# Layer 2's row ends: no transposes back, diagonal and residual in halves beside the cell's gates

## The chip, the cores and the metric

The kernel runs on one core of a Trainium2 chip, as one launch. The metric is the device time of that launch in microseconds (us). The engines are named as in the profile: PE is TensorE (matmuls and transposes; PEld is its loading of weights), DVE is VectorE, ACT is ScalarE, POOL is GpSimd, SP is SyncE, which only issues DMAs here. A name with a q (SPq, ACTq) is an engine's sequencer. All arithmetic is in fp32, apart from some masks in bfloat16.

## The reference

There are N = 2708 nodes with F = 256 features, and a dense matrix `adj` of N x N that has no negative entries and holds about 1% nonzeros. Four graph layers follow one another, and each is wrapped in a residual and a layernorm without gain and offset:

```python
x = layernorm(x + L0(x, adj))          # adj @ (x * W)
x = layernorm(x + L1(x, adj, ...))     # attention with 4 heads of 64
x = layernorm(x + L2(x, adj, adj, ...))
x = layernorm(x + L3(x, adj, ...))
```

The change lies between layers 2 and 3. Cut to what matters, with the branches for negative entries left out:

```python
# L2(h)
dn = de = diag(adj);  A = adj with its diagonal set to 0
edge_output = gru(A @ h, h, edge weights)
support     = mean over 3 heads of softmax(masked scores) * A @ (h @ gat_W)
node_output = gru(support, h, node weights)
return de[:, None] * edge_output + dn[:, None] * node_output
# L3(x)
hn = adj @ (x @ neigh_W.T) / (adj.sum(1, keepdims=True) + 1)
return concatenate([x, hn], axis=-1) @ lin_W.T
```

Layer 3 is linear in x, so it can be written as `x @ L1 + rdeg * (adj @ (x @ L2))`, where L1 is the first half of `lin_W.T`, L2 is `neigh_W.T` times its second half, and rdeg is 1 / (degree + 1). The kernel uses that: `lwn` is the matrix of 256 x 512 that holds L1 and L2 side by side.

## The kernel before

**Tiles.** The nodes lie in NT = 22 row tiles of P = 128 (the last has 20). The features are FC = 2 halves of 128. Two layouts are in use: rows (a node on each partition, 256 features in the free dimension) and transposed (128 features on the partitions, nodes in the free dimension).

**Layer 2's heads.** The output columns are split into two halves h of NH = 1354 nodes, and each of these into three units u of 512, 512 and 330 columns. One unit takes both halves at once. The loop at the end of this section runs over the units, over the K = 3 heads and over the MH = 11 pairs c of row tiles. For each pair, ACT makes the scores `p` with two activations (L1258 and L1261), DVE multiplies them by the block of `adj` (L1262), and `seven` (L298) forms one product of 2 x 2 blocks with seven matmuls in place of eight: DVE makes the sums `s` and `pa` (L304 to L307) for it, and L317 issues the matmuls into seven of the eight PSUM banks. So L317 is the stream that PE works on throughout this stage, from 887 to 1626 us, with two breaks in it for other work at each pair.

**Turns.** After the third and the sixth of the seven matmuls `seven` calls `between` (L291). It runs one step of a Python generator, up to its next `yield`: first from the list `urgent`, and if this is empty, from `later`. One such step is a turn. A unit with 3 x 11 pairs has 66 turns. `project` (L1098, 4 turns for each head) goes into `urgent`; `edge_cells` (L1233) and `node(u, est)` (L1208) go into `later`. So `node(0)` runs in the turns of unit 1's heads, `node(1)` in those of unit 2's, and `node(2)` in those of layer 3's first unit, where some pairs have a turn after each of their seven matmuls. The turns set the order of PE's instructions; on the other engines the order in which the program's lines are reached, together with the Tile scheduler, decides.

**One bank for all turns.** `bank()` (L1057) hands out the one PSUM bank that is left (the pool `ps_f` has one buffer). Each turn takes it, PE writes it, and ACT or DVE must have read it before the next turn's first matmul may start.

**node.** For each half h of a unit (six halves in all):

1. `load_cell` (L1184) loads `xt`, the transposed features of the layer's input, and `et`, the edge cell's output, by DMAs that POOL issues (L246). Each has one buffer. For h = 1 this stands in the loop over the row ends of h = 0.
2. `cell` (L1115) computes the GRU cell, transposed, in 8 turns: for each half j of the features the gates r, h, n and z, each with two or four matmuls (L1128) and one ACT activation out of the bank. The DVE operations that combine the gates stand after the fourth gate, and write `yt`.
3. L1217 adds `et` to `yt` for both halves of features in one DVE operation.
4. `by_tiles` (L1191) cuts the columns into row tiles. A tile that reaches over the border between two stretches of columns is put together by POOL copies (L1201).
5. The row ends take three turns for each of the 22 tiles. `node_rows` (L1152) transposes `yt` back to rows (two PE transposes, L1157); DVE reads the bank, multiplies by the node's diagonal entry and adds the residual `xs` (L1160), and the layernorm follows: statistics on DVE, the power for 1/sqrt on POOL, the normalisation on DVE (L181). `rows_turned` (L1166) transposes the normalised rows again (two PE transposes, L1170), and ACT copies them to `xt` (L1172). `rows_end` (L1175) multiplies them by `lwn` (two matmuls with 512 columns, L1179); ACT copies the second half to `h3` (L1180), DVE adds the first half to the normalised rows (L1181), and POOL issues the DMA that stores this sum as `y3_d` for the end of layer 3.

**Layer 0's stage** prepares `lwn`: `lin_W` and `neigh_W` are transposed, multiplied (L559) and stored to memory; `load_lwn` loads the result ahead of layer 2's heads. `diag`, the diagonal in rows layout (128 x 22), is there from that stage on. The stage that transposes the softmax statistics stands at about 700 to 720 us and writes them to `st_d`.

Of the kernel before, what the change touches and what calls it, by code (L numbers as in the profile page):

```python
# [19 lines left out]
P = 128  # L20
# [7 lines left out]
def kernel(  # L28
# [113 lines left out]

    fall_d = dram.tile([H, N], F32, name="fall_d")
    st_d = [dram.tile([2 * K, 2, W], F32, name=f"st_{u}") for u in range(len(units))]

# [247 lines left out]
    if True:  # L393
# [13 lines left out]
        if True:  # L407
# [39 lines left out]
            with pool("l0", 2) as l0:  # L447
# [48 lines left out]
                with pool("prep", side="right") as prep:  # L496
# [49 lines left out]
                    nw = weights(prep, "nw", neigh_w)  # L546
                    lw = weights(prep, "lw", lin_w)
                    nc.gpsimd.dma_start(lwn_d[:, :, :F], lw[:, :FC])
                    lwn2 = prep.tile([P, FC, F], F32, name="lwn2")
# [6 lines left out]
                    for i in range(FC):  # L556
                        pt = ps_t.tile([P, 4, P], F32, tag="tr", name="pt").rearrange("p i q -> p (i q)")
                        for o in range(FC):
                            nc.tensor.matmul(  # L559
                                pt[:, :F], nwt[:, o, i * P : (i + 1) * P], lw[:, FC + o, :], start=(o == 0), stop=(o == FC - 1)  # L560
                            )
                        nc.scalar.copy(lwn2[:, i], pt[:, :F])
                    nc.gpsimd.dma_start(lwn_d[:, :, F:], lwn2)
                    layer0_mask(ahead, strips[ahead])
# [42 lines left out]
            if True:  # L607
# [350 lines left out]
                next(ahead)  # L958

                for lo in range(0, NT, 4):  # L960
                    hi = min(lo + 4, NT)
# [84 lines left out]
    with (  # L1046
# [67 lines left out]

        def cell(est, xt, yt, w, wih, whh, b):  # L1115

            for j in range(FC):
                got = {}
                for i, nm in ((0, "r"), (2, "h"), (3, "n"), (1, "z")):
# [9 lines left out]
                    if nm == "n":  # L1129
                        nc.scalar.activation(yt[:, j, :w], g[:, :w], AF.Identity, bias=b[:, 3, j : j + 1])  # L1130
                    else:
                        s = nleft.tile([P, W], F32, tag=f"g_{nm}", name=f"g_{nm}")
                        nc.scalar.activation(
                            s[:, :w], g[:, :w], AF.Identity if nm == "h" else AF.Tanh,
                            scale=0.5, bias=b[:, i, j : j + 1],
                        )
                        got[nm] = s
                    yield

# [6 lines left out]
                nc.vector.scalar_tensor_tensor(z, z, 1.0, h, ALU.add, ALU.mult)  # L1146
                nc.vector.scalar_tensor_tensor(n, z, 0.5, r, ALU.mult, ALU.add)


        shared, shared3 = {}, {}  # L1150

        def node_rows(t, src):  # L1152

            n = sz(t)
            pt = bank()
            for f in range(FC):
                nc.tensor.transpose(pt[:n, f * P : (f + 1) * P], src[:, f, :n], ident)  # L1157
            y = nleft.tile([P, F], F32, tag="y", name="y", bufs=3)

            nc.vector.scalar_tensor_tensor(  # L1160
                y[:n], pt[:n, :F], diag[:n, t : t + 1], xs[t][:n], ALU.mult, ALU.add,
            )
            layernorm(y, y, n)
            return t, y

        def rows_turned(t, y):  # L1166
            n = sz(t)
            pt = bank()
            for f in range(FC):
                nc.tensor.transpose(pt[:, f * P : f * P + n], y[:n, f * P : (f + 1) * P], ident[:n, :n])  # L1170
            xt = nleft.tile([P, FC, P], F32, tag="xt", name="xt", bufs=2)
            nc.scalar.copy(xt[:, :, :n], pt.rearrange("p (f q) -> p f q", q=P)[:, :FC, :n])  # L1172
            return t, y, xt

        def rows_end(t, y, xt):  # L1175
            n = sz(t)
            pz = bank()
            for f in range(FC):
                nc.tensor.matmul(pz[:n], xt[:, f, :n], lwn[:, f, :], start=(f == 0), stop=(f == FC - 1))  # L1179
            nc.scalar.copy(h3[t][:n], pz[:n, F:])  # L1180
            nc.vector.tensor_tensor(y[:n], y[:n], pz[:n, :F], ALU.add)  # L1181
            nc.gpsimd.dma_start(y3_d[t], y[:n])

        def load_cell(lo, w):  # L1184
            got = []
            for parts, tag in ((xt_d, "xt2"), (edge_d.values(), "et")):
                got.append(nleft.tile([P, FC, W], F32, tag=tag, name=tag))
                load_columns(got[-1], parts, lo, w, nc.gpsimd)
            return got

        def by_tiles(lo, w, src, ends, among=range(NT)):  # L1191
# [16 lines left out]
        def node(u, est):  # L1208
# [3 lines left out]
            for h in range(2):  # L1212
                lo = h * NH + a
                xt, et = nxt or load_cell(lo, w)
                yt = nleft.tile([P, FC, W], F32, tag="yt", name="yt")
                yield from cell(est[h], xt, yt, w, *node_w, b_node)
                nc.vector.tensor_tensor(yt[:, :, :w], yt[:, :, :w], et[:, :, :w], ALU.add)  # L1217
                tiles = by_tiles(lo, w, lambda at, n: yt[:, :, at : at + n], shared)
                got, turned = [], []
                for i in range(len(tiles) + 2):  # L1220
                    if i < len(tiles):
                        got.append(node_rows(*tiles[i]))
                        yield
                    if i >= 2:
                        rows_end(*turned[i - 2])
                        yield
                    if 0 < i <= len(tiles):
                        turned.append(rows_turned(*got[i - 1]))
                        yield
# [401 lines left out]
```

## Time and profile before

Three runs took 1880.27, 1880.66 and 1879.21 us, a median of 1880.27.

| what | value |
|---|---|
| profiled execution | 1881.39 us |
| its span in the profile | 1879.3 us |
| instructions | 23102 |
| granted TensorE clock | 0.998 of full speed |
| busy PE, 0 to 890 us (layers 0 and 1, edge cells) | 874.5 of 890 us |
| busy PE, 890 to 1180 us (heads of unit 0 and the first of unit 1) | 289.5 of 290 us |
| busy PE, 1180 to 1735 us (heads with row ends among them) | 544.4 of 555 us |
| busy PE, 1735 to 1879 us (layer 3) | 132.2 of 144 us |
| L1157, transposes to rows | 44 matmuls, 1207.9 to 1719.9 us |
| L1170, transposes back | 44 matmuls, 1213.1 to 1729.9 us |
| L1160, DVE, diagonal and residual of a tile | 22 of 0.478 us |
| L181, DVE, normalisation of a tile's rows | 22 of 0.413 us |
| L1172, ACT, copy of the turned rows | 22 of 0.372 us |
| L1181, DVE, sum of the rows and the first half | 22 of 0.416 us |

How to read it: the span is what the profiler recorded between the first and the last instruction, and the time of the execution is longer by what lies around it. The four rows of busy PE come from stretches of the trace. The durations are medians of one instruction in this one execution. A matmul in fp32 shows as two records, and the end of a record is modelled, so the costs of PE are read from starts rather than from durations. Lists that are given as "waiter, releaser" name the instruction that waited, then the one whose end released it.

### The profile page before, as it was taken

Reading aid. Unit: us, or ns where it says so; the run is one execution under the profiler, and the core shown is the slowest. Engines: PE = TensorE matmul, PEld = TensorE weight load, DVE = VectorE, ACT = ScalarE, POOL = GpSimd, SP = SyncE. Lnnn points to the kernel's source line nnn. Section 1 sums busy time; section 2 is a strip of 40 time slices with the busy share of each in tenths; the row PEclk is TensorE's granted clock in tenths of the full one; section 3 lists DMA queues with packets and bytes.
Section 4 is the critical chain, followed back from the end, with each engine's and each line's share of the span. In section 5 each row is a group of like instructions: output and inputs, shape, how many; then the busy total and the mean of one; then the engine's idle time right before and its main releaser. Section 6 shows DMA issues by size and latency. Waiting matters only on the chain.

```text
span 1879.3 us, 23102 instructions
## 1 busy us (share of the span) xinstructions
PE 1840.5 (98%) x7561; PEld 1035.5 (55%) x7565; DVE 1279.0 (68%) x2280; ACT 689.0 (37%) x1419; POOL 259.9 (14%) x419
## 2 busy tenths in 40 slices
PE   8999999999999999999999999999999999999997
PEld 7788842233345886887444444444445555554555
DVE  5343479999897655654658888776887758744664
ACT  4444410033144203111555665555564555311011
POOL 1211220001012411000011001210200202111111
PEclk9999999999999999999999999999999999999999
DMA  9344410100002657764557665454554445534764
GB/s 298 130 146 146 159 42 1 30 1 12 12 7 74 144 143 188 176 144 113 164 148 207 179 168 147 134 155 115 163 144 114 128 103 134 155 101 109 198 167 123
DMA packets 434204, 235.92 MB, mean 126 GB/s; under 512 B 184182, under 2 KB 421388, under 8 KB 431644
## 3 DMA queue, kind: packets, MB, share of 16 engines
q1 hardware_dynamic: 417438, 207.41, 40.5%
q0 software_dynamic: 7760, 21.20, 3.5%
q10 hardware_dynamic: 8878, 5.76, 1.0%
q8 instruction: 62, 1.02, 0.2%
q14 instruction: 66, 0.54, 0.1%
HBM read 221.61 MB, written 12.65 MB: 125 GB/s over the span
## 4 chain that ended last, share of the span: by engine, by line
PE 83%; DMA 5%; DVE 4%; issue 3%; ACT 2%; POOL 1%; SPq 1%; ACTq 0%; DVEq 0%; POOLq 0%
PE m L317 38%; PE acc L763 11%; PE bank L1128 7%; PE acc L211 7%; PE den L772 6%; PE gate L1003 4%; PE bank L1104 3%; DMA strip<-in_adj_t_dram 2%; PE bank L1179 1%; ACT below L465 1%; DMA p<-in_adj_t_dram 1%; SPq L264 1%; PE pm L419 1%; POOL bn_rs L175 1%; PE pq L929 1%
## 5 line engine op out<-in xcount | busy, mean ns | idle before, releaser
L781 DVE SCALAR_TENSOR_TENSOR p<-fall_b,rise,mask 128x1024 f32<-128x1024 f32 (+1 forms) x264 | 294.0, 1157 | 32.5 <-PE den L772 16.7
L1258 ACT ACTIVATE p<-st,e_neg 128x1024 f32<-128x1024 f32 (+1 forms) x198 | 197.1, 1040 | 193.7 <-PE m L317 186.3
L317 PE MATMUL m<-s,xq 128*128 128x512 f32 (+3 forms) x660 | 230.1, 467 | 0.0
L763 PE MATMUL acc<-p,h 128*64 128x512 f32 (+2 forms) x1056 | 214.5, 548 | 0.2 <-ACT sum L794 0.2
L317 PE MATMUL m<-p,xq 128*128 128x512 f32 (+1 forms) x396 | 182.8, 543 | 0.1
L211 PE MATMUL acc<-turn,strip 128*128 128x257 f32 x792 | 181.5, 379 | 0.0
L1261 ACT ACTIVATE p<-p 128x1024 f32<-128x1024 f32 (+1 forms) x198 | 178.9, 943 | 0.2
L1262 DVE TENSOR_TENSOR p<-p,blk 128x1024 f32<-128x1024 f32 (+1 forms) x132 | 143.6, 1107 | 39.7 <-ACT p L1261 24.3
L317 PE MATMUL m<-p,x 128*128 128x512 f32 (+1 forms) x396 | 167.8, 542 | 0.3 <-DVE supt L334 0.3
L304 DVE TENSOR_TENSOR s<-p 128x512 f32<-128x512 f32 (+3 forms) x132 | 81.1, 615 | 124.3 <-PE m L317 101.0
L317 PEld LDWEIGHTS m<-s,xq 128*128 128x128 f32 x660 | 124.3, 190 | 74.8 <-issue 57.6
L211 PEld LDWEIGHTS acc<-turn,strip 128*128 128x128 f32 x792 | 147.2, 190 | 20.3
L763 PEld LDWEIGHTS acc<-p,h 128*64 128x64 f32 x1056 | 69.8, 136 | 138.2 <-issue 128.6
L317 PE MATMUL m<-s,x 128*128 128x512 f32 (+3 forms) x330 | 127.3, 467 | 0.0
L772 PE MATMUL den<-p,h 128*32 128x512 f32 (+2 forms) x1056 | 117.7, 548 | 0.0
L317 PEld LDWEIGHTS m<-p,xq 128*128 128x128 f32 x396 | 74.6, 190 | 76.0 <-issue 61.4
L317 PEld LDWEIGHTS m<-p,x 128*128 128x128 f32 x396 | 74.4, 190 | 73.6 <-issue 61.2
L465 ACT ACTIVATE below<-strip 128x384 bf16<-128x384 f32 x132 | 78.5, 594 | 72.9 <-DMA strip<-in_adj_t_dram 69.5
L1262 DVE TENSOR_TENSOR p<-p,turn 128x1024 f32<-128x1024 f32 (+1 forms) x66 | 72.2, 1108 | 17.9 <-PE m L317 11.6
L305 DVE TENSOR_TENSOR p<-p 128x512 f32<-128x512 f32 (+3 forms) x132 | 82.4, 625 | 1.9
L307 DVE TENSOR_TENSOR s<-p,s 128x512 f32<-128x512 f32 (+3 forms) x132 | 81.5, 617 | 2.0
L317 PEld LDWEIGHTS m<-s,x 128*128 128x128 f32 x330 | 61.8, 190 | 38.1 <-issue 34.3
(276 smaller groups left out, 2541.1 us busy)
## 6 DMA issues: line engine op xcount, KB each, us to landing
strip<-in_adj_t_dram SPq DMA_DIRECT2D x19, 1408.0 KB, 6.0
blk<-in_adj_t_dram SPq DMA_DIRECT2D x88, 256.0 KB, 3.4
blk<-in_adj_t_dram SPq DMA_DIRECT2D x88, 192.0 KB, 4.0
pa<-in_adj_t_dram SPq DMA_DIRECT2D x110, 128.0 KB, 2.7
turn<-in_adj_t_dram SPq DMA_DIRECT2D x44, 256.0 KB, 3.3
blk<-in_adj_t_dram SPq DMA_DIRECT2D x88, 128.0 KB, 2.5
p<-in_adj_t_dram SPq DMA_DIRECT2D x88, 128.0 KB, 2.6
turn<-in_adj_t_dram SPq DMA_DIRECT2D x44, 192.0 KB, 3.1
```

Of the source, the lines that this page charges most:

```text
L211: nc.tensor.matmul(acc, s[:, c, :n], rhs(c), start=(c == 0), stop=(c == NT - 1))
L305: nc.vector.tensor_tensor(a21, a21, a11, ALU.subtract)
L307: nc.vector.tensor_tensor(s4, a12, s2, ALU.subtract)
L317: nc.tensor.matmul(dst[:, :w], lt, rt, start=start and not (one_bank and i), stop=stop and not (one_bank and i in (1, 2, 5)))
L465: nc.scalar.activation(below[:, : (hi - lo) * P], s[:, lo:hi].rearrange("p c n -> p (c n)"), AF.Relu, scale=-1.0, accum_out=negative[:, BE ...
L763: nc.tensor.matmul(acc[s][i * HD : (i + 1) * HD, :ws], hs[c][:, 2 * q + i, :HD], ps[i][:, p0 : p0 + ws], **flags,)
L772: nc.tensor.matmul(den[j : j + CT, :ws], hs[c][:, 2 * q + i, HD + 1 - CT :], ps[i][:, p0 : p0 + ws], **flags,)
L781: nc.vector.scalar_tensor_tensor(p[:, :w], falls[g // 2][:, 2 * q + i, :w], rise[:, c, 2 * q + i : 2 * q + i + 1], mask[:, c, at : at + w] ...
L1128: nc.tensor.matmul(g[:, :w], lt, rt, start=(q == 0), stop=(q == len(terms) - 1))
L1258: nc.scalar.activation(p[:, :, :w], st_k[:, :, :w], AF.Relu, scale=-1.0, bias=e_neg[:, at, k : k + 1])
L1261: nc.scalar.activation(p[:, :, :w], p[:, :, :w], AF.Exp, scale=-1.0)
L1262: nc.vector.tensor_tensor(p[:, :, :w], p[:, :, :w], blk[:, i, :, :w], ALU.mult)
```

## The change

- `cell` takes two functions. `prepare(j)` is called after the gate h of a half j of the features, and multiplies that half of `et` by the diagonal and adds `xt` to it. `rest(j)` is called at the end of the half, and multiplies the half of `yt` by the diagonal and adds that `et`. So residual and diagonal are applied in transposed layout, 128 x 512 (or 330) at a time; L1217 and the DVE operation L1160 go.
- For this the diagonal is needed along the free dimension: it is transposed to a row once, stored to `diag_d`, and loaded for each half, the same on all partitions, as `drow` (one buffer, by POOL's queue).
- One turn between the cell and the row ends does nothing.
- `node_rows` transposes to rows as before, but ACT copies them out of the bank; the statistics are taken from these rows. `rows_turned` is gone: `rows_end` multiplies the slice of `yt`, which has been transposed all along and isn't normalised, by `lwn`. The scale 1/sqrt of a row is applied to the product after it; the mean drops out, because `centred` has taken the mean over the rows from each column of both matrices in `lwn`. Each row tile takes two turns in place of three.

```diff
--- before.py
+++ after.py
@@ -141,6 +141,7 @@
     nc.gpsimd.memset(turn.rearrange("p (t f) -> p t f", f=FE)[:, :, F:], 1.0)
 
     fall_d = dram.tile([H, N], F32, name="fall_d")
+    diag_d = dram.tile([NT, P], F32, name="diag_d")
     st_d = [dram.tile([2 * K, 2, W], F32, name=f"st_{u}") for u in range(len(units))]
 
     y3_d = [dram.tile([sz(t), F], F32, name=f"y3_{t}") for t in range(NT)]
@@ -545,6 +546,16 @@
                         finish(layer0_rest(l0, t))
                     nw = weights(prep, "nw", neigh_w)
                     lw = weights(prep, "lw", lin_w)
+                    minus = prep.tile([P, P], F32, name="minus")
+                    nc.gpsimd.memset(minus, -1.0 / F)
+
+                    def centred(w):
+                        pt = ps_t.tile([P, 4, P], F32, tag="tr", name="pt").rearrange("p i q -> p (i q)")
+                        for f in range(FC):
+                            nc.tensor.matmul(pt[:, :F], minus, w[:, f, :], start=(f == 0), stop=(f == FC - 1))
+                        nc.vector.tensor_tensor(w, w, pt[:, None, :F].to_broadcast([P, FC, F]), ALU.add)
+
+                    centred(lw[:, :FC])
                     nc.gpsimd.dma_start(lwn_d[:, :, :F], lw[:, :FC])
                     lwn2 = prep.tile([P, FC, F], F32, name="lwn2")
                     nwt = prep.tile([P, FC, F], F32, name="nwt")
@@ -560,6 +571,7 @@
                                 pt[:, :F], nwt[:, o, i * P : (i + 1) * P], lw[:, FC + o, :], start=(o == 0), stop=(o == FC - 1)
                             )
                         nc.scalar.copy(lwn2[:, i], pt[:, :F])
+                    centred(lwn2)
                     nc.gpsimd.dma_start(lwn_d[:, :, F:], lwn2)
                     layer0_mask(ahead, strips[ahead])
                     layer0_own(ahead, strips[ahead])
@@ -957,6 +969,11 @@
                 nc.vector.reciprocal(rdeg, rdeg)
                 next(ahead)
 
+                pt = ps_t.tile([P, 4, P], F32, tag="tr", name="pd")
+                nc.tensor.transpose(pt[:NT, 0, :], diag, ident)
+                drows = tail.tile([NT, P], F32, name="drows", bufs=1)
+                nc.scalar.copy(drows, pt[:NT, 0, :])
+                nc.gpsimd.dma_start(diag_d, drows)
                 for lo in range(0, NT, 4):
                     hi = min(lo + 4, NT)
                     at, w = lo * P, width(lo, hi)
@@ -1112,7 +1129,7 @@
                         nc.vector.scalar_tensor_tensor(e, pw[:, :w], 1.0 / K, e, ALU.mult, ALU.add)
                     yield
 
-        def cell(est, xt, yt, w, wih, whh, b):
+        def cell(est, xt, yt, w, wih, whh, b, prepare=None, rest=None):
 
             for j in range(FC):
                 got = {}
@@ -1135,6 +1152,8 @@
                             scale=0.5, bias=b[:, i, j : j + 1],
                         )
                         got[nm] = s
+                    if nm == "h" and prepare:
+                        prepare(j)
                     yield
 
                 r, z, h, n = got["r"][:, :w], got["z"][:, :w], got["h"][:, :w], yt[:, j, :w]
@@ -1145,6 +1164,8 @@
                 nc.vector.tensor_tensor(h, xt[:, j, :w], r, ALU.subtract)
                 nc.vector.scalar_tensor_tensor(z, z, 1.0, h, ALU.add, ALU.mult)
                 nc.vector.scalar_tensor_tensor(n, z, 0.5, r, ALU.mult, ALU.add)
+                if rest:
+                    rest(j)
 
 
         shared, shared3 = {}, {}
@@ -1156,29 +1177,19 @@
             for f in range(FC):
                 nc.tensor.transpose(pt[:n, f * P : (f + 1) * P], src[:, f, :n], ident)
             y = nleft.tile([P, F], F32, tag="y", name="y", bufs=3)
-
-            nc.vector.scalar_tensor_tensor(
-                y[:n], pt[:n, :F], diag[:n, t : t + 1], xs[t][:n], ALU.mult, ALU.add,
-            )
-            layernorm(y, y, n)
-            return t, y
-
-        def rows_turned(t, y):
-            n = sz(t)
-            pt = bank()
-            for f in range(FC):
-                nc.tensor.transpose(pt[:, f * P : f * P + n], y[:n, f * P : (f + 1) * P], ident[:n, :n])
-            xt = nleft.tile([P, FC, P], F32, tag="xt", name="xt", bufs=2)
-            nc.scalar.copy(xt[:, :, :n], pt.rearrange("p (f q) -> p f q", q=P)[:, :FC, :n])
-            return t, y, xt
-
-        def rows_end(t, y, xt):
+            nc.scalar.copy(y[:n], pt[:n, :F])
+            mean, rs = moments(y, n)
+            return t, src, y, mean, rs
+
+        def rows_end(t, src, y, mean, rs):
+
             n = sz(t)
             pz = bank()
             for f in range(FC):
-                nc.tensor.matmul(pz[:n], xt[:, f, :n], lwn[:, f, :], start=(f == 0), stop=(f == FC - 1))
-            nc.scalar.copy(h3[t][:n], pz[:n, F:])
-            nc.vector.tensor_tensor(y[:n], y[:n], pz[:n, :F], ALU.add)
+                nc.tensor.matmul(pz[:n], src[:, f, :n], lwn[:, f, :], start=(f == 0), stop=(f == FC - 1))
+            nc.vector.tensor_scalar(y[:n], y[:n], mean, rs, ALU.subtract, ALU.mult)
+            nc.scalar.activation(h3[t][:n], pz[:n, F:], AF.Copy, scale=rs)
+            nc.vector.scalar_tensor_tensor(y[:n], pz[:n, :F], rs, y[:n], ALU.mult, ALU.add)
             nc.gpsimd.dma_start(y3_d[t], y[:n])
 
         def load_cell(lo, w):
@@ -1187,6 +1198,13 @@
                 got.append(nleft.tile([P, FC, W], F32, tag=tag, name=tag))
                 load_columns(got[-1], parts, lo, w, nc.gpsimd)
             return got
+
+        def load_diag(lo, w):
+
+            dst = nleft.tile([P, W], F32, tag="drow", name="drow")
+            src = bass.AP(tensor=diag_d.tensor, offset=diag_d.offset + lo, ap=[[0, P], [1, w]])
+            nc.gpsimd.dma_start(dst[:, :w], src)
+            return dst
 
         def by_tiles(lo, w, src, ends, among=range(NT)):
 
@@ -1212,20 +1230,32 @@
             for h in range(2):
                 lo = h * NH + a
                 xt, et = nxt or load_cell(lo, w)
+                drow = load_diag(lo, w)
                 yt = nleft.tile([P, FC, W], F32, tag="yt", name="yt")
-                yield from cell(est[h], xt, yt, w, *node_w, b_node)
-                nc.vector.tensor_tensor(yt[:, :, :w], yt[:, :, :w], et[:, :, :w], ALU.add)
+                parts = [[a[:, j, :w] for j in range(FC)] for a in (xt, et, yt)]
+
+                def prepare(j):
+
+                    xj, ej, _ = (a[j] for a in parts)
+                    nc.vector.tensor_tensor(ej, ej, drow[:, :w], ALU.mult)
+                    nc.vector.tensor_tensor(ej, ej, xj, ALU.add)
+
+                def rest(j):
+
+                    _, ej, yj = (a[j] for a in parts)
+                    nc.vector.tensor_tensor(yj, yj, drow[:, :w], ALU.mult)
+                    nc.vector.tensor_tensor(yj, yj, ej, ALU.add)
+
+                yield from cell(est[h], xt, yt, w, *node_w, b_node, prepare, rest)
+                yield
                 tiles = by_tiles(lo, w, lambda at, n: yt[:, :, at : at + n], shared)
-                got, turned = [], []
-                for i in range(len(tiles) + 2):
+                got = []
+                for i in range(len(tiles) + 1):
                     if i < len(tiles):
                         got.append(node_rows(*tiles[i]))
                         yield
-                    if i >= 2:
-                        rows_end(*turned[i - 2])
-                        yield
-                    if 0 < i <= len(tiles):
-                        turned.append(rows_turned(*got[i - 1]))
+                    if i:
+                        rows_end(*got[i - 1])
                         yield
                     if i == 1 and h == 0:
                         nxt = load_cell(NH + a, w)
```

## The prediction

> **What bounds the kernel now.** I read the page first: engine shares, then the chain that ended last.
>
> ```profile
> PE 1840.5 (98%) x7561; PEld 1035.5 (55%) x7565; DVE 1279.0 (68%) x2280; ACT 689.0 (37%) x1419; POOL 259.9 (14%) x419
> ...
> PEclk9999999999999999999999999999999999999999
> ...
> PE 83%; DMA 5%; DVE 4%; issue 3%; ACT 2%; POOL 1%; SPq 1%; ACTq 0%; DVEq 0%; POOLq 0%
> ```
>
> TensorE (PE) is busy in all slices, at full clock, and carries 83% of the chain. What PE streams less, and what it waits less, is what the change can be worth; DVE, ACT and POOL count only where PE waits for them. So the next view is the list of PE's own waits (waiter, releaser, us in total, times, longest):
>
> ```profile
> PE bank L1170 <- DVE y L1181: 3.7, 5, 1.1
> PE m L317 <- DMA p<-in_adj_t_dram: 2.5, 2, 1.6
> PE m L317 <- DVE pa L305: 2.2, 3, 1.2
> PE pm L419 <- ACT xt L189: 1.9, 3, 1.0
> PE bank L1170 <- DVE y L181: 1.9, 3, 1.2
> PE bank L1157 <- POOL yt L1201: 1.3, 2, 1.0
> PE bank L1179 <- DVE y L1160: 1.0, 3, 0.4
> ...
> PE bank L1157 <- DVE yt L1217: 0.2, 1, 0.2
> ```
>
> Five of these eight belong to the row ends: 3.7 + 1.9 + 1.3 + 1.0 + 0.2 = 8.1 us in 14 waits. The timeline shows that a wait costs PE some more: before the wait of 0.71 us at 1223.90 the matmuls at 1222.17 would have streamed until 1223.03 (two records at 0.43 us, the spacing of 512-wide records), so the gap is 0.87, 0.16 more. With that the five cost 8.1 + 14 x 0.16 = 10.3 us.
>
> The timeline of PE gives the price of a pair of transposes in a stream of matmuls, by starts:
>
> ```profile
> 1713.09 0.38 PE L1170 MATMUL bank<-ident,y 128*128 128x128 f32 x2
> 1713.31 0.89 PE L317 MATMUL m<-s,turn 128*128 128x430 f32 x2
> ```
>
> The next matmul starts 0.22 us later, which is the cost; the 0.38 is a modelled end that overlaps. Two stretches by engine (length, PE, PEld, DVE, ACT, POOL, clock, DMA share, GB/s) show the cover on DVE, during a cell and during row ends:
>
> ```profile
> 1440.00:1455.00 15.00, 15.00 (x44) 8.06 (x43) 9.00 (x16) 6.10 (x9) 0.00 (x0) 1.00 0.32 85
> 1320.00:1335.00 15.00, 13.61 (x38) 6.09 (x37) 13.11 (x27) 8.36 (x11) 6.58 (x9) 1.00 0.51 146
> ```
>
> In the cell DVE is free 6.0 of 15 us, in the row ends only 1.9, and there PE is idle 1.4.
>
> **What the Trainium skill says.** Three places bear on this. "Perfetto Trace Analysis", Tensor Engine Instruction: ACT, DVE and GpSimd take their instructions strictly first in, first out. The trace agrees: the add L1181 starts at 1223.43, behind the product L1262 of 1222.30, though ACT left the bank at 1221.02. "PSUM — Partial Sum Buffer", PSUM bank collisions raise a hardware error: two engines must not touch one bank at once, two readers (ACT and DVE) included. All turns here share one bank, and DVE's add waited 14.9 us in all for ACT's copy of the same bank. "VectorE: DVE Perf Modes", The TRN2 errata: an fp32 tensor_tensor of N columns takes (N+151)/0.96 ns, 691 at 512 and 501 at 330; rows of these shapes show 0.69 and 0.50 us.
>
> **The change, part by part.** The instruction order of the built kernel shows what it says: 44 transposes fewer on PE, the same matmuls otherwise, and five added.
>
> *PE streaming.* Removed: 22 pairs of L1170 at 0.22 = -4.8 us. The matmuls with lwn stay 44, with yt as weights in place of xt. Added: four 128x256 matmuls for the centred weights, and one transpose for the diagonal. The four L559 matmuls of the same shape start at 59.92 and the next instruction at 61.72: 1.8 us; the transpose 0.1. PE streams without gaps there, so both are on the path: +1.9. The second added weight (lwn2) waits for ACT's copies behind one strip matmul, and the old L559 follows the DVE add into lw with 4 transposes and a strip matmul (0.87 us) between, against some 1.1 of evacuation: +0.2. The weights landed at 38, long before.
>
> *Waits that go.* The matmul no longer needs the normalised rows: L1170 <- L181 goes, 1.9 + 3 x 0.16 = -2.4. The empty turn puts the product and sum of the cell's last half, and POOL's copies of partial tiles, a turn (1.4 to 3.4 us of matmuls) ahead of the first transposes: L1157 <- L1201 and L1217 go, 1.5 + 3 x 0.16 = -2.0.
>
> *Waits that stay or change name.* The transposed rows leave the bank by an ACT copy (0.37 us as L1172) in place of L1160 (0.48). ACT is less full than DVE, but pairs of 1.04 us exponentials stand before it: of 1.5 us I take half, -0.7, between 0 and -1.5. The bank of the lwn matmul is freed by ACT and then DVE as before; now the next tile's transposes or the next lwn matmul wait for it. 3.7 + 5 x 0.16 = 4.5 us, kept: 0; at best -4.5, at worst +2 more, because this evacuation now needs rs from POOL.
>
> *DVE.* Added 48 elementwise operations (product and sum, before and after, two halves of features, six halves of nodes): 32 x 0.69 + 16 x 0.50 = 30.1 us. Removed: L1217 four times 1.22 and twice 0.84 = 6.6; L1160 22 x 0.47 = 10.3. L1181 as scalar_tensor_tensor costs 22 x 0.06 more. Net about +15 us (with the two weight adds). Those after the gates lie in the cell, where 6 of 15 us are free, and cost nothing; without this cover they would cost their length. Those before it (`et` times the diagonal, plus xt) are queued, for five of six halves, amid the row ends of the half before. There they need `drow` and `et`, loaded by POOL.
>
> *That wait, new.* `drow` and `et` have one buffer each, so their loads go out when the previous half's last sum is done, call it t0. POOL issues drow (0.7 us like the et loads), sometimes two partial copies (1.4), two or three et loads (1.5 to 2.2), and only then the power for rs. The last issue ends by t0+2.9 to 4.4 and begins 0.7 earlier; et loads landed in 2.6 to 6.3 us, 3.3 median: data at about t0+5.5 to 7. In DVE's queue the product stands behind four 0.69 sums, two 1.2 us products and the statistics of one or two tiles: reached at t0+5.8 to 8.5. So mostly there, sometimes 1 to 2 us late, and what is queued behind it (s, p, the bank's evacuation) is late too; PE waits for those. I take +1.5 in all; ends 0 and +7 (five halves x 1.4).
>
> *Small.* The diagonal's row: an ACT copy and one POOL DMA at about 700 us, ahead of the st writes; these are needed only near 890. Hidden. In the statistics stage and around the first gates PE's order shifts by a few matmuls; taken as 0, +-1.
>
> Sum: -4.8 + 1.9 + 0.2 - 2.4 - 2.0 - 0.7 + 0 + 1.5 = -6.3 us. Against the profiled execution (span 1879.3, 1881.4 in all) this is 1875.1; that execution lies 1.1 above the median of the runs, so **1874.0**.
>
> **Rivals.**
> *No change in effect.* The bank stays single and its evacuation was the larger wait; the y transposes' waits come back in front of the next tile's transposes. Then only streaming counts: -4.8 + 1.9 + 0.2 = -2.7, with up to 2 either way: 1876 to 1880. For it: L1181 is the longest of the five. Against it: four of the others lose their cause.
> *Slower: DVE's queue blocks on the prefetched rows.* Place: the first `et` product behind the row statistics in halves two to six. Price: at the slowest landing seen, 6.3 us, data is at t0+8 to 10 against 5.8 to 8.5, a block of 2 to 4 us; DVE has some 1 us spare there, so PE loses 1 to 3 us per half, five times: +5 to +15 in place of the +1.5, 1877.5 to 1887.5, about 1885 if the loads are slowed as a rule. It makes the kernel slower than before once it exceeds 1.6 us a half. For it: the row ends are DVE's fullest stretch. Against it: DMA is about half busy there.
> *More than forecast.* With fewer turns, the bank waits after lwn go as well, and nothing blocks: -6.3 - 1.5 - 4.5 - 0.8 = -13.1, 1867.
>
> **How the numbers follow.** Forecast 0.46, none in effect 0.20, slower 0.26, more 0.08. The likeliest one's own range is 1870 to 1877. About 0.2%, 3.8 us, is what a measurement can tell from no change: faster 0.54, same 0.20, slower 0.26. The range from 1868 to 1885 takes the unknown costs in and leaves out about 0.15.
>
> **What would show it.** PE has 44 records fewer named bank<-ident,y and its list of waits has no line that ends in the normalisation; the total of the bank waits by row ends falls from 8.1 to 4 to 6 us. The wrong turn would be seen as DVE waiting for a DMA into et or drow for over 5 us in all, or PE's matmul m waiting for DVE s or p between 1210 and 1730, where it now hardly does. If ACT holds the bank, a line bank <- ACT y takes the place of L1160's.

## The result and the profile after

Nine runs of the changed kernel took 1875.7 us in the median (1874.1 to 1878.8), nine of the kernel before 1880.27. The ratio is 0.9979 with a 95% interval of 0.9971 to 0.9987: 2.4 to 5.5 us faster. The forecast was 1874.0, 6.3 us faster, which is more than that interval holds.

The page of the changed kernel, busy time by engine:

```profile
PE 1833.9 (98%) x7530; PEld 1033.8 (55%) x7530; DVE 1295.4 (69%) x2302; ACT 691.6 (37%) x1420; POOL 262.0 (14%) x427
```

PE has 6.6 us less to do, DVE 16.4 more. PE's own waits, in the same view as before (waiter, releaser, us in total, times, longest); L1178 are the transposes to rows, L1192 is DVE's last operation on a tile, L1219 POOL's copy of partial tiles:

```profile
PE bank L1178 <- DVE y L1192: 5.8, 5, 1.8
PE m L318 <- DMA p<-in_adj_t_dram: 2.8, 2, 1.4
PE m L318 <- DVE pa L306: 2.7, 4, 1.2
...
PE bank L1178 <- POOL yt L1219: 1.8, 2, 1.6
```

The row ends now hold PE up for 5.8 + 1.8 = 7.6 us in 7 waits, where it was 8.1 in 14. Three of the five old lines are gone: those on the normalisation, on L1160 and on L1217. The one on POOL's copies has grown from 1.3 to 1.8, and the one on the bank of the `lwn` matmul from 3.7 to 5.8; it now stands in front of the next tile's transposes to rows.

Where the time of the two profiled executions (spans 1879.3 and 1874.9) went, by the starts of the same instructions (rounded one by one):

| stretch | before | changed | difference |
|---|---|---|---|
| start to the first matmul of `project` | 998.8 | 999.2 | +0.4 |
| from there to the last transposes of layer 3 | 865.2 | 858.2 | -7.0 |
| from there to the end of the span | 15.3 | 17.4 | +2.1 |
| sum | 1879.3 | 1874.9 | -4.5 |

So the work with row ends in it gained 7.0 us, and 2.1 came back at the very end. Of the 7.0, nothing is idle time of PE. The same stretch by engine (length, PE, PEld, DVE, ACT, POOL, clock, DMA share, GB/s), before and changed:

```profile
998.81:1864.01 865.20, 853.02 (x2395) 434.44 (x2394) 619.44 (x1064) 378.87 (x484) 119.21 (x183) 1.00 0.53 144
```

```profile
999.25:1857.48 858.23, 846.01 (x2351) 431.31 (x2351) 633.86 (x1084) 380.50 (x484) 120.67 (x188) 1.00 0.54 146
```

PE stands idle for 865.2 - 853.0 = 12.2 us before and for 858.2 - 846.0 = 12.2 us after, and is busy for 7.0 us less. The 22 pairs of transposes account for 4.8 of these. Seven waits fewer, at the 0.16 us that the prediction found beside each wait, may account for 1.1 (an estimate; this part of a wait is covered by the modelled end of a matmul and counts as busy). About 1.1 us stays open.

The end of the span has nothing of the change in it. After the last activation the kernel stores its last tile, and the engines meet in a barrier. SP's waits in the last 9 us, before and changed (L1627 and L1657 are the launch, after the kernel's last line):

```profile
SPq L1627 <- PEq L1627: 0.7, 2, 0.5
```

```profile
SPq L1657 <- PEq L1657: 2.9, 2, 2.4
```

The barrier takes 2.2 us longer. The section on the hardware comes back to it.

Two of the long waits in detail. The timeline of DVE (start, duration, operation, and in brackets the idle time before it with its releaser) around the one that ends at 1480.88:

```profile
1478.21 0.69 DVE L1240 TENSOR_TENSOR et<-et,drow 128x512 f32<-128x512 f32 x1 [1.23 <-DMA et<-edget]
1478.82 0.41 DVE L1190 TENSOR_SCALAR y<-y,bn_mv,bn_rs 128x256 f32<-128x256 f32 x1
1479.14 0.69 DVE L1241 TENSOR_TENSOR et<-et,xt 128x512 f32<-128x512 f32 x1
1479.75 0.69 DVE L1240 TENSOR_TENSOR et<-et,drow 128x512 f32<-128x512 f32 x1
1480.35 0.48 DVE L1192 SCALAR_TENSOR_TENSOR y<-bank,bn_rs,y 128x256 f32<-128x256 f32 x1
```

DVE stands idle for 1.23 us until `et` has landed, does three operations for the next cell, and only then empties the bank (L1192), for which PE has waited 1.83 us. Nothing at this place needs `et` soon: the sum that reads it (L1247) starts at 1528.6. In the program these operations stand behind all row ends of this half, so it was the scheduler that put them here.

The five waits on L1192 can all be followed like this. In each, ACT had left the bank 1.0 to 3.3 us before L1192 started, and L1192 started straight behind another DVE operation, so it is DVE's queue that held the bank. In three of the five, which make 3.2 of the 5.8 us, operations on `et` stand in that queue. In the other two (1.8 and 0.8 us) there is none: the stream's products and sums stand there, L1292 above all, and 0.44 us each time in which DVE waits for the power on POOL.

For the other of the two waits, POOL's timeline shows why the empty turn didn't cover the partial copies:

```profile
1547.29 1.02 POOL L276 TENSOR_TENSOR blk<-blk,offdiag 128x128 f32<-128x128 f32 x2 [4.13 <-DMA blk<-in_adj_t_dram]
1548.26 0.58 POOL L1206 DMA_DIRECT2D drow<-diag_d  x1
1548.85 1.04 POOL L1219 COPY yt<-yt 128x108 f32<-128x108 f32 x2
```

Two clearings of a block and the issue of the next `drow` stand in POOL's queue ahead of the copies, 1.6 us together. PE waited 1.55.

### The profile page after: what moved, and what is told of

It is laid out like the page before. It is cut to its first block, busy times and chain, and to the rows that moved or that the text cites. A ratio compares the mean times of both kernels' runs of the same rounds, so it can differ in the third digit from the quotient of the medians.

```text
span 1874.9 us, 23105 instructions
## 1 busy us (share of the span) xinstructions
PE 1833.9 (98%) x7530; PEld 1033.8 (55%) x7530; DVE 1295.4 (69%) x2302; ACT 691.6 (37%) x1420; POOL 262.0 (14%) x427
## 3 DMA queue, kind: packets, MB, share of 16 engines
q8 instruction: 62, 1.02, 0.2%
## 5 line engine op out<-in xcount | busy, mean ns | idle before, releaser
L1292 DVE TENSOR_TENSOR p<-p,blk 128x1024 f32<-128x1024 f32 (+1 forms) x132 | 143.0, 1103 | 32.6 <-ACT p L1291 21.9
L276 POOL TENSOR_TENSOR blk<-blk,offdiag 128x128 f32<-128x128 f32 (+3 forms) x50 | 30.8, 621 | 371.9 <-DMA blk<-in_adj_t_dram 208.3
```

Source lines behind the costliest of these rows:

```text
L1292: nc.vector.tensor_tensor(p[:, :, :w], p[:, :, :w], blk[:, i, :, :w], ALU.mult)
```

## The experiments

Times are compared as ratios to runs of the kernel before on the same chip; the last column is the ratio's distance from 1, times 1880.27 us. The difference between two of these lines is less sure than either: 2 to 3 us to both sides, an estimate from the two intervals.

| run | ratio, 95% interval | us |
|---|---|---|
| changed kernel | 0.9979 (0.9971 to 0.9987) | -3.9 |
| e1_no_turn | 0.9975 (0.9965 to 0.9986) | -4.7 |
| e2_halves_only | 1.0022 (1.0015 to 1.0029) | +4.1 |
| e3_turn_only | 1.0003 (0.9994 to 1.0011) | +0.6 |
| e4_no_centre | 0.9974 (0.9963 to 0.9984) | -4.9 |
| e5_pool_fewer | 0.9974 (0.9964 to 0.9984) | -4.9 |
| e6_late | 0.9951 (0.9937 to 0.9965) | -9.2 |
| e7_early | 0.9970 (0.9958 to 0.9982) | -5.6 |
| e8_identity | 0.9922 (0.9908 to 0.9935) | -14.7 |
| e9_identity_late | 0.9927 (0.9913 to 0.9940) | -13.7 |
| e10_identity_late_act | 0.9908 (0.9895 to 0.9921) | -17.3 |
| e11_twice | 1.0007 (0.9999 to 1.0016) | +1.3 |
| e12_before_identity | 0.9988 (0.9979 to 0.9996) | -2.3 |

### The parts alone

**The empty turn**, taken out of the changed kernel (e1) and put alone into the kernel before (e3):

```diff
                 yield from cell(est[h], xt, yt, w, *node_w, b_node, prepare, rest)
-                yield
```

> The changed kernel without the empty turn; all else is the same, and the turns after the cell move one place forward. The prediction's account: the turn takes the waits for the cell's last sum and for POOL's partial copies off PE, worth 2.0 us, so this run is 2.0 slower than the changed kernel (about 1877.7 against 1875.7) and PE waits of bank <- yt L1218 or L1247 grow from 1.8 to about 4. Rival: the changed kernel still shows PE waiting 1.8 us for a partial copy, so the turn brought nothing: within 0.7 us of the changed kernel.

> The kernel before with nothing but the empty turn between cell and row ends. The prediction's account: the waits L1157 <- L1201 and L1217 go, 2.0 us faster than before. Rival: the turn is only one place later for all that follows; within 0.7 us of before.

e3's interval has no room for a gain of 2.0 us, and e1 is no slower than the changed kernel, where 2.0 us would have put it at 0.9990. The turn is worth nothing that can be seen. In e1 the copies hold PE up for 1.0 us in place of 1.8. In e3 the wait for POOL's copies falls from 1.3 to 0.3 us and the one for L1217 stays at 0.2, but L1170 <- L1181 grows from 3.7 to 4.9. e3 is the weaker of the two tests: there the old sum L1217 stands behind the empty turn, and in the changed kernel the cell's last sum stands ahead of it.

**The halves**, without the removal of the transposes:

```diff
-            mean, rs = moments(y, n)
-            return t, src, y, mean, rs
+            layernorm(y, y, n)
+            return t, y
+
+        def rows_turned(t, y):
...
-        def rows_end(t, src, y, mean, rs):
+        def rows_end(t, y, xt):
...
-                nc.tensor.matmul(pz[:n], src[:, f, :n], lwn[:, f, :], start=(f == 0), stop=(f == FC - 1))
+                nc.tensor.matmul(pz[:n], xt[:, f, :n], lwn[:, f, :], start=(f == 0), stop=(f == FC - 1))
...
```

> Diagonal and residual in halves and the empty turn, as in the changed kernel, but the row ends normalise and transpose back as before, and the weights are not centred. The two turned-row buffers lie in the gates' tiles. The prediction's account: of the 6.3 us, the transposes back carry 5.1 (4.8 streaming, 2.4 waits, less 2.1 for the centring), and this part only 1.2: about 1.2 faster than before, 3.4 slower than the changed kernel as measured. Rival A: DVE's added 15 us cost; 1 to 4 us slower than before, and the transposes carry 6 to 8. Rival B: halves carry most: 3 us or more faster than before.

4.1 us slower than before, 2.8 at least: rival A. The halves cost, and the rest of the change, above all taking the transposes out, gains about 8 us on top of them. PE's waits show a part of it:

```profile
PE bank L1186 <- DVE y L1198: 7.4, 6, 2.3
```

L1198 is the old sum L1181, and the wait for it has doubled from 3.7 us. L1186 are the transposes back. The other waits of the row ends shrank, so in this trace the stretch from the first `project` to the last transposes is only 1.9 us longer than before (867.1 against 865.2). The rest of the difference lies ahead of `project`, in a stretch whose length goes from 998.8 to 1002.5 us over the fourteen traces, and isn't explained. One thing here differs from both kernels: the turned rows lie in the gates' tiles, for want of room, which may cost something too.

**The centring**:

```diff
-                    centred(lw[:, :FC])
...
-                    centred(lwn2)
```

> The changed kernel without the subtraction of column means in layer 0's stage (the mean of the rows is then not taken out of the product). The prediction's account: four matmuls and their waits on the path, 1.8 to 2.0 us faster than the changed kernel. Rival: the two traces reach the first matmul of layer 1 (252.1 and 252.3 us) and the end of layer 0's strips (242.7 and 243.0) only 0.2 to 0.3 us apart, so that stage's waits for strips hide the four matmuls: at most 0.5 us faster.

0.9 us faster than the changed kernel, which the intervals don't separate from zero, nor from 2.0. The traces say more, because the centring lies ahead of layer 1. The first matmul of layer 1 starts at 250.9 to 253.8 us in the nine traces with the centring (252.4 in the mean) and at 251.4 to 252.8 in the five without it (252.1). So it cost about 0.3 us, or up to about 1.2 by the scatter of the traces (an estimate), but not 2.1. That waits for strips hide the rest fits, but no run here shows it.

**A pair of transposes**, doubled:

```diff
+            for f in range(FC):
+                nc.tensor.transpose(pt[:n, F + f * P : F + (f + 1) * P], src[:, f, :n], ident)
```

> The changed kernel with each pair of transposes to rows done a second time, into the unused half of the same bank (nothing reads it): 22 pairs more on PE, in the same turns. The prediction's price of a pair, 0.22 us: 4.8 us slower than the changed kernel. Rival: the second pair delays ACT's copy and all behind it, more than 6 us; or it is hidden in waits, less than 3.

0.0028 more than the changed kernel, 5.3 us, with 2.2 to both sides, so the rival of more than 6 isn't shut out by the time alone. The timeline of PE shows the price directly (L1178 the pair, L1180 the second one):

```profile
1313.45 0.38 PE L1178 MATMUL bank<-ident,yt 128*128 128x128 f32 x2
1313.67 0.38 PE L1180 MATMUL bank<-ident,yt 128*128 128x128 f32 x2
1313.89 1.02 PE L318 MATMUL m<-s,x 128*128 128x512 f32 x2
```

From start to start 0.22 us, twice. So the price stands, and 22 x 0.22 = 4.8 with it. The wait on DVE's last operation rose as well in this trace, from 5.8 to 7.0 us.

### What holds the bank

**Operations on et queued behind their own gates** (e6). `issue_after` fixes DVE's order and adds no wait:

```diff
-                    if nm == "h" and prepare:
-                        prepare(j)
...
-                nc.vector.scalar_tensor_tensor(r, r, 1.0, h, ALU.add, ALU.mult)
+                first = nc.vector.scalar_tensor_tensor(r, r, 1.0, h, ALU.add, ALU.mult)
...
+                if prepare:
+                    with tc.issue_after(first.ins):
+                        prepare(j)
```

> The changed kernel with the product and sum on et queued on DVE behind the first DVE operation of the same gates, so that they no longer stand among the row ends of the half before. The prediction's account: that wait was worth 1.5 us in all: 1.5 faster than the changed kernel, with the waits L1178 <- L1192 at 4 in place of 5.8. Rival, DVE blocked by prefetched rows: 3 or more faster. Other rival: the operations only move to the end of the cell, where what follows waits for them: not faster.

The interval lies wholly below the changed kernel's, 5.3 us faster between the middles. The wait at 1480 is gone, and most of the line with it, from 5.8 to 0.8, while a wait of the stream for DVE has grown from 0.3 us (L1193 is the old L1192):

```profile
PE m L318 <- DVE p L306: 2.2, 2, 1.8
...
PE bank L1179 <- DVE y L1193: 0.8, 1, 0.8
```

Not all of the 5.0 us is the order's: one of the changed kernel's waits that are gone here, 1.8 us, had no operation on `et` in front of it. And the trace is of an execution of 1877.6 us, where the median of the five is 1874.0. In the stretch from the first `project` to the last transposes PE idles 9.0 us in place of 12.2, but is busy for 849.0 in place of 846.0, so this one execution shows the waits gone and no gain in time. The 5.3 us rest on the times alone.

**The bank emptied without rs** (e7):

```diff
-            nc.vector.tensor_scalar(y[:n], y[:n], mean, rs, ALU.subtract, ALU.mult)
-            nc.scalar.activation(h3[t][:n], pz[:n, F:], AF.Copy, scale=rs)
-            nc.vector.scalar_tensor_tensor(y[:n], pz[:n, :F], rs, y[:n], ALU.mult, ALU.add)
+            nc.scalar.copy(h3[t][:n], pz[:n, F:])
+            nc.vector.scalar_tensor_tensor(y[:n], y[:n], mean, pz[:n, :F], ALU.subtract, ALU.add)
+            nc.scalar.activation(h3[t][:n], h3[t][:n], AF.Copy, scale=rs)
+            nc.vector.tensor_scalar(y[:n], y[:n], rs, None, ALU.mult)
```

> The changed kernel with the bank of the lwn matmul emptied without rs: ACT copies h3 unscaled, DVE forms (y - mean) + product, and both are scaled in SBUF afterwards (one ACT pass more). Theory, the bank now waits for the power on POOL: the waits L1178 <- L1192 fall from 5.8 to 3 or less, 2 to 3 us faster than the changed kernel. Rival, what holds the bank is DVE's place in its queue: within 1 us.

1.7 us faster, not to be told from the changed kernel, and the wait still stands at 4.3 us in 3 waits. Together with the five waits above, where L1192 each time stood behind another DVE operation, this says that it is mostly not rs but DVE's queue.

**The identity in the weights** (e8). With 1 added on the diagonal of the first half of `lwn`, ahead of the centring, the product already holds the rows less their mean:

```diff
+                    for f in range(FC):
+                        nc.vector.tensor_tensor(lw[:, f, f * P : (f + 1) * P], lw[:, f, f * P : (f + 1) * P], ident, ALU.add)
                     centred(lw[:, :FC])
...
-            nc.vector.tensor_scalar(y[:n], y[:n], mean, rs, ALU.subtract, ALU.mult)
             nc.scalar.activation(h3[t][:n], pz[:n, F:], AF.Copy, scale=rs)
-            nc.vector.scalar_tensor_tensor(y[:n], pz[:n, :F], rs, y[:n], ALU.mult, ALU.add)
+            nc.scalar.activation(y[:n], pz[:n, :F], AF.Copy, scale=rs)
```

> The changed kernel with the identity added to the first half of lwn before the centring, so that the product is already rows minus mean plus product: ACT alone empties the bank, in two scaled passes, and DVE's two operations per tile (0.41 + 0.48 us, 22 times, 19.6 us) go. Theory, DVE's queue holds the bank: the waits L1178 <- y fall from 5.8 to 2 or less and DVE's other waits fall too, 4 to 5 us faster than the changed kernel. Rival, rs on POOL holds it: ACT now waits for it and holds up the exponentials, within 1.5 us of the changed kernel or slower.

14.7 us faster than before, 10.7 faster than the changed kernel, more than was expected. PE's waits:

```profile
PE m L318 <- DVE pa L306: 2.3, 4, 1.2
PE m L318 <- DMA p<-in_adj_t_dram: 2.2, 2, 1.7
PE bank L1180 <- POOL yt L1220: 1.7, 2, 1.5
PE m L318 <- DVE p L306: 1.4, 2, 0.9
```

No wait of the row ends on DVE for the bank is left. In its trace the stretch from the first `project` to the last transposes takes 851.2 us, 7.0 less than in the changed kernel, and PE idles in it for 6.7 us in place of 12.2. The stream's own waits for DVE haven't fallen (2.3 + 1.4 us here, 2.7 + 0.3 there), so it isn't DVE's lighter load in general. The end of the span is short again (6.5 us from the last activation in place of 8.2), which makes 8.8 of the 10.7; 1.8 of these lie at the end of the span and not at the bank.

**Both** (e9), and the partial tiles copied by ACT on top (e10):

```diff
-                    nc.gpsimd.tensor_copy(ends[t][:, :, c0:c1], got)
+                    (nc.scalar.copy if ends is shared else nc.gpsimd.tensor_copy)(ends[t][:, :, c0:c1], got)
```

> Both edits of e6_late and e8_identity: the identity in lwn, and the operations on et queued behind the first DVE operation of their own gates. Theory, both gains come from one cause, DVE's queue in front of the bank: with the identity no DVE operation reads that bank any more, so late brings little on top: ratio to before 0.991 to 0.993, as e8_identity's 0.9922. Rival, the gains add (0.9922 and 0.9951 against the changed kernel's 0.9979): 0.989 to 0.990.

> e9_identity_late with the partial tiles copied by ACT in place of POOL. e8_identity still shows PE waiting 1.7 us in 2 waits for POOL's copy, which stands behind two clearings of blocks and a load on POOL. Theory: these waits go, 1.5 to 2 us faster than e9_identity_late, no line bank <- POOL yt in PE's waits. Rival: ACT's copies stand behind pairs of exponentials, no gain.

e9 is no faster than e8: once DVE doesn't read the bank, what else DVE does ahead of it no longer shows. The rival's sum, 0.989 to 0.990, lies below e9's interval, so the gain of e6 is for the most part contained in that of e8. e10 is the fastest here, 17.3 us faster than before. Its wait for POOL's copies (1.6 us in e9) is gone, and the medians lie 2.3 us apart, though the intervals of e9 and e10 overlap.

**The identity in the kernel before** (e12; L1181 becomes an ACT copy):

```diff
...
+                    for f in range(FC):
+                        nc.vector.tensor_tensor(lw[:, f, f * P : (f + 1) * P], lw[:, f, f * P : (f + 1) * P], ident, ALU.add)
...
-            nc.vector.tensor_tensor(y[:n], y[:n], pz[:n, :F], ALU.add)
+            nc.scalar.copy(y[:n], pz[:n, :F])
```

> The kernel before, with the identity added to the first half of lwn and the sum L1181 on DVE replaced by an ACT copy: the bank of the lwn matmul is emptied by ACT alone, and 22 x 0.42 us leave DVE. Theory, DVE's queue in front of the bank is a cost of the kernel before too: L1170 <- L1181, 3.7 us in 5 waits, goes: 4 to 5 us faster than before. Rival: in the kernel before the waits move to L1160 and L181, which stay: within 2 us of before.

2.3 us, between the two, and the interval (0.8 to 3.9 us) takes in the rival but not the theory: the line L1170 <- L1181 is gone, but the transposes back still wait for DVE's normalisation (1.9) and the `lwn` matmul for L1160's successor (1.2). These two are what the change removes, which fits that the identity is worth more after it.

### The end of the span

> The changed kernel with six instructions that POOL issues long before the rows (three fills, the two stores of the weights for layer 3, the store of the diagonal's row) given to DVE, SP and ACT. They are in places where nothing waits for POOL. Theory: in the changed kernel the stretch from the last store's activation to the end of the span is 8.2 us against 6.1 before, and an eighth fetch of code falls there; POOL has 13 more instructions than before (385 against 372 rows; 381 with the short end, 384 with the long one), so with 379 it is short again: 2.1 us faster than the changed kernel. Rival: the end's length hangs on PE's shorter program: no change, the end stays 8.2.

```diff
-    nc.gpsimd.memset(u_all, 0.0)
+    nc.vector.memset(u_all, 0.0)
...
-                        nc.gpsimd.dma_start(lwn_d[:, :, :F], lw[:, :FC])
+                        nc.sync.dma_start(lwn_d[:, :, :F], lw[:, :FC])
...
```

No gain to be seen, and 8.1 us at the end: six POOL instructions fewer were not enough, or it isn't these. The rival falls as well: e8 leaves the changed kernel's PE program as it is and ends in 6.5 us.

## Why the prediction was right, and where its steps were not

The time was inside the range and the direction was right. Against -6.3, the measured difference was -4.6 by the medians and -3.9 by the ratio. The streaming part was right as it stood. The waits were not: the prediction's own sign was that the waits of the row ends fall from 8.1 to 4 to 6 us, and they fell to 7.6. The waits for the normalisation went (1.9 us), and about as much (2.1) came back in front of the next tile's transposes, which is what the rival "no change in effect" said of them. That the sum came near has luck in it: the centring cost less than was put down, and the end of the program, of which nobody had thought, cost as much as the centring was to cost.

- **PE streaming, -4.8**: right; the price of a pair shows again in e11's timeline.
- **Waits for the normalisation, -2.4**: right, the line is gone.
- **The empty turn, -2.0**: wrong. The step said that the turn puts POOL's copies ahead of the first transposes. In the program `by_tiles` stands behind the empty turn, in the same step as these transposes; POOL's queue had 1.6 us of other issues and clearings before the copies, the new `drow` load among them, and 1.8 us of wait stayed. e1 and e3 give the turn nothing.
- **Transposed rows by ACT, -0.7**: the line L1179 <- L1160 went whole, 1.0 us in 3 waits; at the prediction's 0.16 for each that is -1.5, the far end of its bounds. No line on ACT took its place.
- **The bank of the lwn matmul and the new wait for `et`, 0 and +1.5**: the two are for the most part one. 4.5 us kept and 1.5 new were taken for 6.0 us; 5.8 + 5 x 0.16 = 6.6 were found, all in the line on L1192, and 3.2 of the 5.8 us stand behind operations on `et`. The size was nearly right; the path was not, because DVE waited only 2.3 us for `et`, in 3 waits, and it is the operations themselves, put ahead of L1192, that hold the bank. The rival "slower" named the right queue; it put up to 15 us on it, and only one of the long waits, with DVE idle for 1.23 us, shows it as it was drawn.
- **DVE's added operations "cost nothing" in the cell**: half wrong. In the changed kernel no line of PE's waits ends in those after the gates. But alone, the halves made the kernel 4.1 us slower where the prediction's terms for them gave 1.2 faster, and the rest brought 8 where the terms gave 5.1. The sum hid both. In the traces, inside the stretch with row ends, the halves cost 1.9 us and the rest gained 8.9, of which the end of the program took 1.9 back.
- **The centring, +2.1**: mis-sized; about 0.3 by the traces.
- **The end of the program**: not thought of, +2.1.

The corrected sum is -4.8 + 0.3 - 2.4 + 0 - 1.5 + 2.1 + 2.1 = -4.2, against -4.5 between the two spans; of the two terms of +2.1 the first is the bank (6.6 - 4.5) and the second the end. That it comes so near proves little: the stretch ahead of `project` alone differs by up to 3.7 us between traces.

## What to carry to other kernels

Where one buffer is passed from turn to turn, ask for each reader what stands in front of it on its engine, before asking how long it takes: here an engine that is idle for 31% of the span held PE up because its order put the next cell's work first. An addition can sometimes be folded into the weights of a matmul that is there anyway, and so leave a full engine's queue; that was worth 10.7 us on top of the change, 8.9 without the short end of the span, and only 2.3 in the kernel before. A step that makes room by a pause can do nothing if the queue it waits for is filled again by what the pause lets in. And a list of waits in which lines vanish isn't a gain yet: here the sum of PE's idle time stayed at 12.2 us.

## What the hardware did that was not expected

**The end of the span has two lengths.** From the start of the last activation to the end it took 6.0 to 6.5 us in seven of the fourteen kernels here and 8.0 to 8.4 in the other seven. It isn't the number of code fetches that fall there: there are 7 before, 8 in the changed kernel, and 8 in e10, which ends in 6.2 us.

```profile
q14 instruction: 8, 0.07, 2.9%
```

```profile
q14 instruction: 8, 0.07, 3.6%
```

(The DMA view of the last 8.2 us of the changed kernel and of the last 6.3 us of e10: transfers, MB, share.) The traces show where the difference lies: on POOL, between its last branch and the next record of its sequencer. These two, before and then changed (durations in ns, first and last start in us):

```profile
L1584 POOLq COMPARE_BRANCH  x1: 50/50/50, 1873.0 to 1873.0; - x1
L1584 POOLq EVENT_SEMAPHORE  x1: 17/17/17, 1873.5 to 1873.5; - x1
```

```profile
L1614 POOLq COMPARE_BRANCH  x1: 50/50/50, 1866.4 to 1866.4; - x1
L1614 POOLq EVENT_SEMAPHORE  x1: 17/17/17, 1869.2 to 1869.2; - x1
```

From start to start that is 0.5 us in all seven short ones and 2.6 to 2.9 us in all seven long ones. The Trainium skill ("Runtime: NRT & Kernel Launch", Instruction fetch mechanics) says that a taken branch out of the window of code that an engine holds makes the engine wait until the target's block is fetched. This kernel ends with a branch past the code for negative entries, so a pause behind it fits. The same section gives the blocks as 16 KiB, 256 instructions; over the whole span of the changed kernel q14 moved 0.55 MB in 67 transfers, 8.2 KB each, and only q8 moved 16 KB at a time (62 transfers, 1.02 MB), so the page's block isn't the one on q14. What makes the pause long is open. The records of POOL and its sequencer divide the two kinds (745 to 760 in the short ones, 767 to 775 in the long ones), but those of DVE do so too (3331 to 3373 and 3385 to 3409), and no run here moved one of these numbers alone.

**The power on POOL takes 0.54 us, or up to 2.06.** The longest in the changed kernel's trace stands beside two DVE operations that each read two tensors:

```profile
1316.13 1.21 DVE L1292 TENSOR_TENSOR p<-p,blk 128x1024 f32<-128x1024 f32 x1
1317.27 0.68 DVE L308 TENSOR_TENSOR s<-p,s 128x512 f32<-128x512 f32 x1
```

```profile
1316.29 2.06 POOL L176 TENSOR_TENSOR bn_rs<-bn_rs,neg_half 128x1 f32<-128x1 f32 x1 [2.79 <-DVE bn_rs L175]
```

It ends 0.40 us after the second of them. "GPSIMD Engine Reference" of the Trainium skill, Specifications, says that POOL shares its way into SBUF with DVE and contends with DVE instructions that have two SBUF inputs. The trace agrees: of its 66 powers, the 49 that overlap such a DVE operation by less than 0.05 us take 0.57 us at most, and every one that takes more than 0.6 us overlaps such operations, by 0.3 to 1.7 us. In e8's trace one took 3.87 us. In the changed kernel this cost little: DVE stood idle for only 0.44 us until the longest power was done.
